# A Perceiver block on one core: the context's product for batches 2 to 14 by Strassen's scheme, with work moved between the vector engines

## The chip, the cores and the metric

The kernel runs on one core of a Trainium2 chip. The core has a matrix engine (TensorE, PE in the profile; its weight loads are PEld), three engines for element-wise work (VectorE or DVE, ScalarE or ACT, GpSimd or POOL), and SyncE (SP), which here only issues transfers. Each engine runs its own instructions in order; they wait for one another through semaphores. Matrix products read SBUF and write to PSUM, which has eight banks of 128 partitions x 512 float32 values. The metric is the time of one execution on the device in microseconds.

## The reference

Sixteen batches of 128 tokens with 512 features pass three stages; each adds to x what it makes of the normalised x. All is float32.

```python
# 1: cross-attention on the batch's own context, 2048 rows x 512
h      = layernorm(x)
probs  = softmax(h @ ctx.T)              # (128, 2048)
x      = x + probs @ ctx                 # "the context's product"
# 2: causal self-attention, 16 heads of 32; down- and up-projections, rotary half
x      = x + attention(layernorm(x), Wq, Wk, Wv) @ Wc
# 3: two of eight experts of rank 64, chosen by the first token
h      = layernorm(x)
x      = x + h + gates-weighted (h @ A.T) @ B.T
```

## The kernel before

**Tiling.** A batch is one tile of 128 tokens. The context of a batch is cut in four pieces v of 512 rows, and each piece in four chunks j of 128 rows. Both the context (`ctx`, rows on partitions) and its transpose (`ctxT`, features on partitions) are loaded for each piece, 1 MB each, by `load_ctx` and `load_turned`. The scores are made turned: `score` (L247) multiplies chunks of `ctxT` with the turned norm rows `hT` into a PSUM bank `psc`, so that context rows are on partitions and tokens along the bank. `keep_score` (L258) copies the bank to `sc` on ScalarE and keeps the running maximum `mx` on VectorE. `turn_max`, `most` and `spread` (L274 to 287) make from it the maximum of each token and spread it over the partitions with TensorE; `less` (L289) adds its negative on VectorE and `power` (L295) takes the exponential on ScalarE. `sums` (L298) adds the powers of each token, `whole` and `portion` finish the denominator. `attend` (L308) is the context's product: for each v, four matmuls with `sc` of a chunk (128 x 128) as weights and the chunk of `ctx` (128 x 512) as moving operand, all sixteen accumulated in one bank `av`. `x1_of` (L326) divides and adds x.

**Norms.** `Norm.moments` takes mean and variance on VectorE (`bn_stats`, `bn_aggr`) and the reciprocal root on POOL; `rows` applies them on VectorE; `turned` transposes 32x32 blocks on VectorE and sends the tile through DRAM and back (`d`, `hT`, on SP), which finishes the transposition.

**Self-attention.** `project` makes q and k, `rotate` and `rotated` apply the rotary part (VectorE and POOL), `project_v` makes v from the tokens in another order (`order_tokens`, POOL), `compare` makes the scores of all heads in four banks `pss` with row groups of 32, `powers` masks them, takes the maximum (VectorE) and the exponential with its sum (ScalarE, one instruction a head), `divided` divides on POOL, `turn_probs` transposes in 32x32 pieces on VectorE into `pT`, `heads` multiplies with v (`y`, four column groups of 32) and `join` with Wc (`o`). **Experts.** `shares`, `logit` and `choose` pick two experts, `fetch` gathers their weights by indirect transfers issued on POOL, `middle` (`mid`, weights of 64 columns for the two experts in turn) and `widen` (`ffn`) multiply, `end` adds and writes out.

**Order.** Every instruction is kept in program order (the class `InOrder`, L95), so each engine's queue is what the loop of L694 writes down. One pass of it handles three batches at once: self-attention of batch b, cross-attention's second half (less to x1) of a = b + 1, scores of s = b + 2, and the experts of l = b - 1. The order on TensorE in one pass is: q, spread, q, k, v, av (v = 0), pss, av, lg, av, den, av, psc, mid, psc, psc, ffn, y, psc, o. The last two batches are written out behind the loop.

**PSUM.** The eight banks are split in pools: `ps_sc` two, `ps_av` one, `ps_acc` five, each used in turn. All operations that go through `InOrder` carry line 101 in the profile, so they are told apart by the names of their tiles.

Of the kernel before, what the change touches and what calls it, by code (L numbers as in the profile page):

```python
# [66 lines left out]
def perceiver_block(ctx: ExitStack, tc: tile.TileContext, io: dict, out: bass.AP):  # L67
# [8 lines left out]
    ps_av = ctx.enter_context(tc.tile_pool(name="ps_av", bufs=1, space=PSUM))  # L76
    ps_acc = ctx.enter_context(tc.tile_pool(name="ps_acc", bufs=5, space=PSUM))
# [43 lines left out]
    class Norm:  # L121
        def __init__(self, src, name, n=P, tag="h", mixed=False, hT=None):
            self.src, self.name, self.n, self.tag, self.mixed, self.hT = src, name, n, tag, mixed, hT

        def moments(self):
            n = self.n
            stats = p2.tile([P, 6], F32, tag="stats", name=f"st_{self.name}")[:n]
            dve.bn_stats(stats, self.src)
            self.mv = p2.tile([P, 2], F32, tag="mv", name=f"mv_{self.name}")[:n]
            dve.bn_aggr(self.mv, stats)  # L130
            self.rstd = p2.tile([P, 1], F32, tag="rstd", name=f"rs_{self.name}")[:n]
            pool.tensor_scalar_add(self.rstd, self.mv[:, 1:2], EPS)
            pool.tensor_tensor(self.rstd, self.rstd, mhalf[:n], ALU.pow)
            return self

        def rows(self):
            of = p2 if self.tag == "h" else p1
            self.h = of.tile([P, D], F32, tag=self.tag, name=f"{self.tag}_{self.name}")[: self.n]
            to, of = self.h, self.src
            if self.mixed:  # L140
                to = to.rearrange("p (c a j) -> p c a j", c=KC, j=Q)
                of = of.rearrange("p (c j a) -> p c a j", c=KC, j=Q)
            dve.tensor_scalar(to, of, self.mv[:, 0:1], self.rstd, ALU.subtract, ALU.mult)
            return self
# [89 lines left out]
    norms, hTs = {}, {}  # L234
    scs, mxs, psc, parts, dens, rdens, avs, spreads, trs = ({} for _ in range(9))
# [3 lines left out]
    def norm1(b):  # L239
        norms[1, b] = Norm(xs[b], f"1_{b}", mixed=early(b), hT=(p2, "hT1")).moments()  # L240
# [6 lines left out]
    def score(b, v):  # L247
        ct, hT = turned_cts.pop((b, v)), hTs[1, b]
        ps = bank(ps_sc, "sc", f"psc_{b}_{v}").rearrange("p (j t) -> p j t", j=4)
        for j in range(4):  # L250
            for c in range(KC):
                matmul(
                    ps[:, j, :], ct[:, c, j * P : (j + 1) * P], hT[:, :, c, :],
                    start=(c == 0), stop=(c == KC - 1),
                )
        psc[b, v] = ps

    def keep_score(b, v):  # L258
        if v == 0:
            scs[b] = p2.tile([P, VC, 4, S], F32, tag="sc", name=f"sc_{b}")  # L260
            mxs[b] = p1.tile([P, 4, S], F32, tag="mx", name=f"mx_{b}")
        sc, mx, ps = scs[b], mxs[b], psc.pop((b, v))
        act.copy(sc[:, v], ps)
        if v:
            dve.tensor_tensor(mx, ps, mx if v > 1 else sc[:, 0], ALU.max)
        if v == VC - 1:
            dve.tensor_tensor(mx[:, :2], mx[:, :2], mx[:, 2:], ALU.max)
            dve.tensor_tensor(mx[:, 0], mx[:, 0], mx[:, 1], ALU.max)
# [5 lines left out]
    def turn_max(b):  # L274
        trs[b] = bank(ps_acc, "acc", f"tr_m_{b}")
        transpose(trs[b][:, :S], mxs.pop(b)[:, 0], ident)

    def most(b):
        nm = p2.tile([P, 1], F32, tag="nm", name=f"nm_{b}")
        dve.tensor_reduce(nm, trs.pop(b)[:, :S], AX.X, ALU.max, negate=True)  # L280
        diag = p1.tile([P, S], F32, tag="diag", name=f"diag_{b}")
        dve.tensor_scalar(diag, ident, nm, None, ALU.mult)
        trs[b] = diag
# [14 lines left out]
    def sums(b, by=dve):  # L298
        sc = scs[b]
        t = p1.tile([P, 4, S], F32, tag="sums", name=f"sums_{b}")  # L300
        for v in range(1, VC):
            by.tensor_tensor(t, sc[:, v], t if v > 1 else sc[:, 0], ALU.add)
        part = p2.tile([P, S], F32, tag="part", name=f"part_{b}")
        by.tensor_tensor(t[:, :2], t[:, :2], t[:, 2:], ALU.add)
        by.tensor_tensor(part, t[:, 0], t[:, 1], ALU.add)
        parts[b] = part

    def attend(b, v):  # L308
        sc, ct = scs[b], cts.pop((b, v))
        if v == 0:  # L310
            avs[b] = bank(ps_av, "av", f"av_{b}")
        for j in range(4):
            matmul(
                avs[b], sc[:, v, j, :], ct[:, j, :],
                start=(v == 0 and j == 0), stop=(v == VC - 1 and j == 3),
            )
# [9 lines left out]
    def x1_of(b):  # L326
        x1s[b] = p2.tile([P, D], F32, tag="x1", name=f"x1_{b}")
        dve.scalar_tensor_tensor(x1s[b], avs.pop(b), rdens.pop(b), xs.pop(b), ALU.mult, ALU.add)
        norms[2, b] = Norm(x1s[b], f"2_{b}", mixed=b in (0, B - 1), hT=(p1, "hT2")).moments()
# [33 lines left out]
    def order_tokens(b):  # L363
        hTvs[b] = p1.tile([P, KC, S], F32, tag="hTv", name=f"hTv_{b}")
        pool.tensor_copy(
            hTvs[b].rearrange("p c (i b) -> p c i b", i=Q),
            hTs[2, b].rearrange("p i c b -> p c i b"),
        )
# [8 lines left out]
    def keep_v(b):  # L377
        values[b] = p2.tile([P, D], F32, tag="vv", name=f"vv_{b}")
        act.copy(values[b], projected.pop(("v", b)))

    def compare(b):
        qT, kT = turned_qk.pop(("q", b)), turned_qk.pop(("k", b))
        pss = [bank(ps_acc, "acc", f"pss_{b}_{j}") for j in range(4)]
# [14 lines left out]
    def powers(b, g):  # L398
        att, nmx, sm, rsm, pss = atts[b]
        hs = slice(4 * g, 4 * g + 4)  # L400
        dve.tensor_tensor(
            att[:, hs, :],
            pss[g].rearrange("p (h t) -> p h t", h=4),
            cst[:, None, C_MASK : C_MASK + S].to_broadcast([P, 4, S]),
            ALU.add,
        )
        dve.tensor_reduce(nmx[:, hs], att[:, hs, :], AX.X, ALU.max)
        dve.tensor_scalar_mul(nmx[:, hs], nmx[:, hs], -SCALE)
        for i in range(hs.start, hs.stop):
            act.activation(  # L410
                att[:, i, :], att[:, i, :], AF.Exp,
                bias=nmx[:, i : i + 1], scale=SCALE, accum_out=sm[:, i : i + 1],
# [49 lines left out]
    def x2_of(b):  # L462
        x2s[b] = p2.tile([P, D], F32, tag="x2", name=f"x2_{b}")
        dve.tensor_tensor(x2s[b], os_.pop(b), x1s[b], ALU.add)
        norms[3, b] = Norm(x2s[b], f"3_{b}", mixed=late(b), hT=(p2, "hT3")).moments()
# [50 lines left out]
    def fetch(b):  # L516
        blocks, picked, ex = chosen[b]
        spare = b == B - 1
        each = (p2 if spare else p1).tile(
            [P, TOP, KC * R], F32, tag="sc" if spare else "each", name=f"each_{b}"  # L520
# [6 lines left out]
        wb = p2.tile([P, D], F32, tag="wb", name=f"wb_{b}")  # L527
# [15 lines left out]

    state = {}
# [13 lines left out]
    def first_joined(b):  # L558
# [3 lines left out]
        row = p1.tile([1, D], F32, tag="sums", name=f"row_{b}")  # L562
# [131 lines left out]
    for b in range(B - 2):  # L694
        l, a, s = b - 1, b + 1, b + 2
        if b:
            turn_max(a)
            project(b, "q", [0])
            most(a)
            x2_of(l)  # L700
            spread(a)
            project(b, "q", [1, 2, 3])
            order_tokens(b)
            less(a, 0)
            power(a, 0)
            rows(3, l)
            turn(3, l)
            less(a, 1)
            power(a, 1)
            residual(l)  # L710
            load_x(s + 1)
            load_turned(s, 2)
            less(a, 2)
            power(a, 2)
        else:
            project(b, "q")
        rotate(b, "q")
        project(b, "k")
        if b:
            less(a, 3)  # L720
            power(a, 3)
            load_turned(s, 3)
        rotated(b, "q")
        rotate(b, "k")
        project_v(b)
        keep_v(b)
        rotated(b, "k")
        attend(a, 0)
        load_ctx(a + 1, 0)
        compare(b)  # L730
        if b:
            sums(a)
            shares(l)
        powers(b, 0)
        attend(a, 1)
        load_ctx(a + 1, 1)
        powers(b, 1)
        if b:
            logit(l)
            choose(l)  # L740
        divided(b, 0)
        if b:
            fetch(l)
        attend(a, 2)
        powers(b, 2)
        divided(b, 1)
        whole(a)
        portion(a)
        powers(b, 3)
        divided(b, 2)  # L750
        if b:
            gate(l)
        load_ctx(a + 1, 2)
        attend(a, 3)
        divided(b, 3)
        x1_of(a)
        score(s, 0)
        turn_probs(b, 0)
        rows(2, a)
        turn(2, a)  # L760
        keep_score(s, 0)
        if b:
            middle(l)
        for i in (1, 2):
            turn_probs(b, i)
        score(s, 1)
        turn_probs(b, 3)
        keep_score(s, 1)
        load_ctx(a + 1, 3)
        score(s, 2)  # L770
# [3 lines left out]
        load_turned(s + 1, 0)  # L774
        heads(b)
        keep_heads(b)
        keep_score(s, 2)
        score(s, 3)
        if s + 1 < B:
            norm1(s + 1)  # L780
        load_turned(s + 1, 1)
        if s + 1 < B:
            rows(1, s + 1)
            turn(1, s + 1)
# [6 lines left out]
    project(y, "q", [0])  # L791
    most(z)
    x2_of(l)
    spread(z)
    project(y, "q", [1, 2, 3])
    order_tokens(y)
    less(z, 0)
    power(z, 0)
    rows(3, l)
    turn(3, l)  # L800
    for v in (1, 2, 3):
        less(z, v)
        power(z, v)
# [140 lines left out]
```

## Time and profile before

| | |
|---|---|
| median of three runs | 811.38 us (811.08 to 811.56) |
| profiled execution | 812.89 us |
| its span, first to last instruction | 811.1 us |
| granted TensorE clock over the span | 0.995 |
| PE, DVE, ACT, POOL busy in one batch of the loop (a window of 48 us) | 48.0, 37.0, 13.2, 14.5 us |
| HBM read and written | 165.5 and 15.2 MB |

Busy time is the time in which an engine executes something. A float32 matmul appears as two rows[...], so counts of PE are twice those of the source. A group's line gives the operation, what it writes and reads, its shape and count, then the busy time and the mean of one in ns, then the idle time of the engine just before it. In the chain of work that ended last, each piece has its start, its length, and how many rows it has.

### The profile page before, as it was taken

To read this page: it belongs to the slowest core of one execution; us is meant where nothing else is said; L and a number is where in the kernel's file an instruction comes from. 1 tells how busy PE (TensorE), PEld (TensorE's weight loads), DVE (VectorE), ACT (ScalarE), POOL (GpSimd) and SP (SyncE) were. 2 spreads that over 40 slices of the span, in tenths; PEclk is the share of its full clock that TensorE was granted. 3 is DMA by queue.
4 is the path that set the end of the run, shared out by engine and by line. 5 is a ranking of instruction groups with operands and counts; after the bars stand their busy time and mean duration, and the time that the engine had idled before them with its cause. 6 is when DMAs were issued, how large, how long until landed. Compare 5 with 4: busy or idle time off the path is not lost.

```text
span 811.1 us, 14245 instructions
## 1 busy us (share of the span) xinstructions
PE 793.7 (98%) x5506; PEld 570.6 (70%) x5506; DVE 581.7 (72%) x1289; ACT 223.6 (28%) x731; POOL 233.6 (29%) x295
## 2 busy tenths in 40 slices
PE   8999999999999999999999999999999999999985
PEld 8946785858677586867858686785868768586743
DVE  1446777787887778778777877877787777767673
ACT  1222323132142313214231321423132141313341
POOL 2001224133232403323240332324123232305333
PEclk9999999999999999999999999999999999999998
DMA  9989557567565856646585674658566565720001
GB/s 353 389 314 407 223 202 295 221 246 271 179 228 203 288 221 241 269 179 218 211 298 220 227 277 166 230 210 306 216 224 265 197 213 212 296 93 27 27 27 65
DMA packets 57971, 181.61 MB, mean 224 GB/s; under 512 B 5504, under 2 KB 27392, under 8 KB 41520
## 3 DMA queue, kind: packets, MB, share of 16 engines
q1 hardware_dynamic: 53760, 168.38, 55.9%
q0 software_dynamic: 4000, 12.26, 4.0%
q8 instruction: 43, 0.70, 0.3%
q14 instruction: 24, 0.20, 0.1%
q10 hardware_dynamic: 144, 0.07, 0.0%
HBM read 165.48 MB, written 15.20 MB: 223 GB/s over the span
## 4 chain that ended last, share of the span: by engine, by line
PE 96%; DVE 2%; DMA 1%; issue 0%; ACT 0%; POOL 0%; DVEq 0%; ACTq 0%
PE psc L101 29%; PE av L101 28%; PE q L101 7%; PE k L101 7%; PE o L101 7%; PE v L101 6%; PE pss L101 2%; PE mid L101 2%; PE ffn L101 2%; PE y L101 2%; PE spread L101 1%; PE tr L101 0%; PE tr_p L101 0%; DVE h L101 0%; DMA each<-in_A_dram,g_blocks 0%
## 5 line engine op out<-in xcount | busy, mean ns | idle before, releaser
L101 PEld LDWEIGHTS psc<-hT,ctxT 128*128 128x128 f32 x2048 | 234.7, 193 | 12.8 <-issue 9.1
L101 PE MATMUL psc<-hT,ctxT 128*128 128x128 f32 x2048 | 240.2, 277 | 0.7 <-ACT hT L101 0.7
L101 PE MATMUL av<-ctx,sc 128*128 128x512 f32 x512 | 232.9, 600 | 0.0
L101 PEld LDWEIGHTS av<-ctx,sc 128*128 128x128 f32 x512 | 93.6, 190 | 102.1 <-issue 100.3
L101 ACT ACTIVATE att<-att,nmx 128x128 f32<-128x128 f32 x256 | 99.2, 389 | 116.9 <-DVE nmx L101 114.6
L101 POOL TENSOR_TENSOR att<-att,rsm 128x512 f32<-128x512 f32 x60 | 61.2, 1041 | 166.3 <-DVE rsm L101 166.0
L101 DVE STREAM_TRANSPOSE pT<-att 32x512 f32<-32x512 f32 x140 | 98.3, 702 | 12.2 <-POOL att L101 10.3
L101 ACT COPY sc<-psc 128x512 f32<-128x512 f32 x64 | 37.6, 587 | 159.0 <-PE psc L101 159.0
L101 ACT ACTIVATE sc<-sc 128x512 f32<-128x512 f32 x64 | 39.7, 631 | 134.9 <-DVE sc L101 134.9
L101 POOL TENSOR_SCALAR rs<-mv 128x1 f32<-128x1 f32 x48 | 10.8, 226 | 185.4 <-DVE mv L101 183.6
L101 PEld LDWEIGHTS q<-hT,w_q 128*128 128x128 f32 x512 | 59.6, 192 | 4.1 <-issue 4.0
L101 PE MATMUL q<-hT,w_q 128*128 128x128 f32 x512 | 62.2, 275 | 0.0
L101 PE MATMUL k<-hT,w_k 128*128 128x128 f32 x512 | 59.8, 275 | 0.0
L101 PEld LDWEIGHTS k<-hT,w_k 128*128 128x128 f32 x512 | 58.5, 192 | 0.0
L101 PE MATMUL o<-w_c,yT 128*128 128x512 f32 x128 | 57.9, 594 | 0.0
L101 PE MATMUL v<-w_v,hTv 128*128 128x512 f32 x128 | 57.7, 593 | 0.0
L101 DVE TENSOR_TENSOR att<-pss,cst 128x512 f32<-128x512 f32 x64 | 43.3, 677 | 18.1 <-PE pss L101 18.1
L101 DVE TENSOR_SCALAR h<-x,mv,rs 128x512 f32<-128x512 f32 x48 | 33.0, 688 | 27.1 <-POOL rs L101 27.1
L101 POOL DMA_DIRECT2D out_dram<-x x14 | 9.2, 659 | 136.7 <-DVE x L101 136.7
L101 ACT ACTIVATION_READ_ACCUMULATOR att<-att,nmx 128x1 f32 x256 | 47.8, 187 | 0.0
L101 DVE TENSOR_REDUCE nmx<-att 128x4 f32<-128x512 f32 x64 | 43.9, 686 | 2.2
L101 DVE TENSOR_TENSOR mx<-psc,mx 128x512 f32<-128x512 f32 x32 | 21.6, 675 | 30.7 <-ACT sc L101 30.7
(132 smaller groups left out, 830.8 us busy)
## 6 DMA issues: line engine op xcount, KB each, us to landing
ctxT<-in_ctxT_dram SPq DMA_DIRECT2D x64, 1024.0 KB
ctx<-in_ctx_dram SPq DMA_DIRECT2D x64, 1024.0 KB
d<-turn SPq DMA_DIRECT2D x42, 256.0 KB
hT<-d SPq DMA_DIRECT2D x42, 256.0 KB
x<-in_x_dram SPq DMA_DIRECT2D x16, 256.0 KB
out_dram<-x POOLq DMA_DIRECT2D x14, 256.0 KB, 5.4
down_q<-in_Wq_downT_dram SPq DMA_DIRECT2D x2, 1024.0 KB
down_k<-in_Wk_downT_dram SPq DMA_DIRECT2D x2, 1024.0 KB
```

The costliest lines, as they stand in the source:

```text
L101: return lambda *args, **kwargs: tc.keep_in_program_order(issue(*args, **kwargs))
```

## The change

The product of batches 2 to 14 (`by_halves`) is computed by a Strassen-like scheme with seven products in place of eight. The tokens are cut in halves of 64, each v's rows in halves of 256 (two chunks each), the features in halves of 256. `context_halves` makes, on POOL, four differences of 128x512 for each v: one in place in `ctx`, three in a new tile `more`. `token_halves` makes four combinations of `sc` in a tile `blocks`, three on VectorE and one on POOL, for all four v at once. `attend_halves` issues fourteen matmuls for a v with 64 columns of weights and 256 moving columns, alternating between PSUM partitions 0 to 63 and 64 to 127 of two banks; part 0 needs no `blocks`, part 1 does. `attended` and `joined` put the parts together: three copies of half the partitions on ScalarE and five additions on VectorE. Batches 0, 1 and 15 keep the old product.

Beside it: norm rows of most batches are applied on ScalarE (`by_act`, with a shift made on POOL), the diagonal of `most` and the copy of `order_tokens` go to ScalarE, the folds of `mx` and the sums of the powers are one `tensor_reduce` each, the scaling of the maxima in `powers` goes into `scalar_tensor_tensor` and `negate`. PSUM is split anew (`ps_av` two, `ps_acc` four; two of the `pss` banks come from `ps_sc`), `sc`, `vv`, `part` and `wb` have one buffer in place of two, and the order of a pass is written anew: v is followed at once by pss; all of av comes behind it, in the pieces seen below; shares, fetch, residual and the turn of norm 3 come later in the pass.

```diff
     def keep_score(b, v):
         if v == VC - 1:
-            dve.tensor_tensor(mx[:, :2], mx[:, :2], mx[:, 2:], ALU.max)
-            dve.tensor_tensor(mx[:, 0], mx[:, 0], mx[:, 1], ALU.max)
+            most = p1.tile([P, S], F32, tag="most", name=f"most_{b}")
+            dve.tensor_reduce(most, mx.rearrange("p j t -> p t j"), AX.X, ALU.max)
     def rows(self):
+            if self.by_act:
+                act.activation(to, of, AF.Identity, bias=self.shift, scale=self.rstd)
+                return self
     def sums(b, by=dve):
+        if by is dve:
+            dve.tensor_reduce(part, sc.rearrange("p v j t -> p t (v j)"), AX.X, ALU.add)
+            return
+    HT, HD = S // 2, D // 2
+    def by_halves(b):
+        return 1 < b < B - 1
+    def context_halves(b, v, by=pool):
+        b11, b12, b21, b22 = (ct[:, 2 * k : 2 * k + 2, n * HD : (n + 1) * HD] for k in (0, 1) for n in (0, 1))
+        more = p4.tile([P, 3, 2, HD], F32, tag="more", name=f"more_{b}_{v}")
+        by.tensor_tensor(more[:, 1], b22, b12, ALU.subtract)
+        by.tensor_tensor(b12, b12, b11, ALU.subtract)
+        by.tensor_tensor(more[:, 0], b22, b12, ALU.subtract)
+        by.tensor_tensor(more[:, 2], b21, more[:, 0], ALU.subtract)
+    def token_halves(b):
+        t = p1.tile([P, 4, VC, 2, HT], F32, tag="blocks", name=f"blocks_{b}")
+        dve.tensor_tensor(t[:, 0], a21, a22, ALU.add)
+        dve.tensor_tensor(t[:, 2], a11, a21, ALU.subtract)
+        dve.tensor_tensor(t[:, 1], t[:, 0], a11, ALU.subtract)
+        pool.tensor_tensor(t[:, 3], a12, t[:, 1], ALU.subtract)
+    def attend_halves(b, v, parts=(0, 1)):
+        if 0 in parts:
+            of_k = [(
+                (low, left, one, sc[:, v, k, low], ct[:, k, left]),
+                (high, left, two, sc[:, v, 2 + k, high], more[:, 2, k]),
+            ) for k in range(2)]
+        if 1 in parts:
+            of_k += [(
+                (low, left, two, sc[:, v, 2 + k, low], ct[:, 2 + k, left]),
+                (high, left, one, t[:, 1, v, k], more[:, 0, k]),
+                (low, right, two, t[:, 3, v, k], ct[:, 2 + k, right]),
+                (high, right, two, t[:, 0, v, k], ct[:, k, right]),
+            ) for k in range(2)]
...
+    def joined(b):
+        dve.tensor_tensor(e[HT:, 0], one[HT:, :HD], moved[HT:, 0], ALU.add)
+        dve.tensor_tensor(moved[HT:, 1], one[HT:, HD:], moved[HT:, 1], ALU.add)
+        dve.tensor_tensor(e[HT:, 1], two[HT:, HD:], e[HT:, 0], ALU.add)
+        act.copy(first[:HT, 1], e[HT:, 1])
+        dve.tensor_tensor(
+            first[HT:], e[HT:, :1].to_broadcast([HT, 2, HD]),
+            moved[HT:, 1:].to_broadcast([HT, 2, HD]), ALU.add,
+        )
+        dve.tensor_tensor(e, two.rearrange("p (n d) -> p n d", n=2), first, ALU.add)
     def powers(b, g):
-        dve.tensor_tensor(
+        dve.scalar_tensor_tensor(
...
-        dve.tensor_reduce(nmx[:, hs], att[:, hs, :], AX.X, ALU.max)
-        dve.tensor_scalar_mul(nmx[:, hs], nmx[:, hs], -SCALE)
+        dve.tensor_reduce(nmx[:, hs], att[:, hs, :], AX.X, ALU.max, negate=True)
```

The order of a pass after the change, cut to what the steps below speak of:

```python
project(b, "k"); rotate(b, "k"); turn(3, l); project_v(b); rotated(b, "q"); rotated(b, "k")
compare(b)
attend(a, 0, (0,)); attend(a, 1, (0,)); token_halves(a); context_halves(a, 3)
powers(b, 0); attend(a, 0, (1,)); powers(b, 1); divided(b, 0); powers(b, 2); shares(l); divided(b, 1)
attend(a, 1, (1,)); logit(l); powers(b, 3); load_ctx(a + 1, 0); load_ctx(a + 1, 1)
choose(l); divided(b, 2); sums(a); attend(a, 2); load_ctx(a + 1, 2); divided(b, 3)
fetch(l); residual(l); gate(l); attend(a, 3); load_ctx(a + 1, 3); whole(a); attended(a)
turn_probs(b, 0); turn_probs(b, 1); joined(a); portion(a); x1_of(a); norm1(s + 1); score(s, 0)
turn_probs(b, 2); rows(2, a); turn(2, a); score(s, 1); turn_probs(b, 3); rows(1, s + 1); turn(1, s + 1)
context_halves(a + 1, 0); context_halves(a + 1, 1); score(s, 2); middle(l); score(s, 3, [0, 1])
heads(b); widen(l); end(l); keep_heads(b); context_halves(a + 1, 2); score(s, 3, [2, 3]); join(b)
```

## The prediction

> **What bounds the kernel now.** First the head of the page and its chain of work that ended last.
>
> ```profile
> PE 793.7 (98%) x5506; PEld 570.6 (70%) x5506; DVE 581.7 (72%) x1289; ACT 223.6 (28%) x731; POOL 233.6 (29%) x295
> PE 96%; DVE 2%; DMA 1%; issue 0%; ACT 0%; POOL 0%; DVEq 0%; ACTq 0%
> PE psc L101 29%; PE av L101 28%; PE q L101 7%; PE k L101 7%; PE o L101 7%; PE v L101 6%; PE pss L101 2%; PE mid L101 2%; PE ffn L101 2%; PE y L101 2%; PE spread L101 1%; PE tr L101 0%; PE tr_p L101 0%; DVE h L101 0%; DMA each<-in_A_dram,g_blocks 0%
> ```
>
> TensorE is the chain for 96% of the span, and the context's product, av, is 28% of it. So what av takes less is gained, if nobody else becomes late. Second, the same chain in order of time for one batch of the loop, and the line of the windows for it (PE, PEld, DVE, ACT, POOL busy us; clock):
>
> ```profile
> 427.50 7.34 PE psc L101 x64
> 435.71 1.01 PE y L101 x32
> 447.90 3.57 PE k L101 x32
> 451.48 3.44 PE v L101 x8
> 454.91 3.43 PE av L101 x8
> 458.35 1.10 PE pss L101 x32
> 459.45 3.63 PE av L101 x8
> 463.20 3.54 PE av L101 x8
> 466.85 3.54 PE av L101 x8
> 470.39 3.57 PE psc L101 x32
> 473.96 1.02 PE mid L101 x16
> 474.99 1.09 PE psc L101 x8
> 427.00:475.00 48.00, 48.00 (x340) 34.65 (x336) 37.03 (x82) 13.15 (x45) 14.47 (x18) 1.00 0.63 231
> ```
>
> A batch takes 474.99 - 427.50 = 47.49 us, without a gap on PE, at full clock. One float32 matmul is two rows here: 32 rows of k in 3.57 us is 0.1116 us for a row of 128 columns, 8 rows of v in 3.44 is 0.430 for 512; on the line between them a row of 256 takes 0.2177.
>
> **The change on TensorE.** Before, one v of av is 8 rows of 128x512: 8 x 0.430 = 3.44. After, it is 14 matmuls with 64 columns of weights and 256 moving ones, 28 rows. Alone, 28 x 0.2177 = 6.10. But they alternate between the lower and the upper 64 PSUM partitions, and mid, which does the same (64-column weights, alternating i), shows what that gives: 16 rows in 1.02 us, where 16 x 0.1116 one after another would be 1.79, and two at a time 0.89. y, with four groups of 32 columns and a different moving operand in each, does 32 rows in 1.01 (0.89 four at a time). So two streams with different moving operands do run together: 14 x 0.2177 = 3.05 for a v. Saved: 4 x (3.44 - 3.05) = 1.56 us a batch.
>
> Against it stands a rule of the Trainium skill, "TensorEngine Tiling (Array Packing)", Key Properties: changing the tiling mode drains TensorE. The row: mid's 1.02 less 0.89 is 0.13 for one excursion in and out. The new order has two more (halves of v 0 and 1, then lg in full width, then v 2 and 3, then den): +0.26. By a full drain with the next weights loaded bare it could be twice that, 0.52 (one more 0.13 each); I take the row. PE alone: 47.49 - 1.56 + 0.26 = 46.19 a batch.
>
> **The change on the other engines, per batch.** DVE, from the rows:
>
> ```profile
> L101 DVE TENSOR_REDUCE nmx<-att 128x4 f32<-128x512 f32 x64 | 43.9, 686 | 2.2
> L101 DVE TENSOR_SCALAR h<-x,mv,rs 128x512 f32<-128x512 f32 x48 | 33.0, 688 | 27.1 <-POOL rs L101 27.1
> L101 DVE TENSOR_TENSOR sums<-sc,sums 128x512 f32<-128x512 f32 x30 | 20.8, 692 | 3.0
> L101 DVE TENSOR_TENSOR mx<-mx 128x256 f32<-128x256 f32 x16 | 6.8, 425 | 0.6
> L101 POOL TENSOR_TENSOR qP<-qP,cst 128x512 f32<-128x512 f32 x15 | 19.1, 1272 | 21.0 <-DVE qP L101 21.0
> L101 POOL TENSOR_TENSOR sums<-sc,sums 128x512 f32<-128x512 f32 x2 | 2.9, 1432 | 0.2
> ```
>
> Away: three norm rows 2.07, diag 0.29, the folds of mx 0.42 + 0.29, of sums 0.68 + 2 x 0.69 + 0.42 + 0.29, four scalings of nmx 4 x 0.17: 6.5. Added: token_halves 3 x 0.69, joined 3 x 0.42 (64x256, by the 256-element row) + 2 x 0.69, the reduce of mx 0.69, the reduce of sums over 2048 elements, and 4 x 0.07 for scalar_tensor_tensor (750 ns beside tensor_tensor's 677). A reduce of 2048 has no row: 686 ns is some 0.15 fixed and 0.53 for 512, so 2.3; strided reading has none either, and twice, 4.5, is my upper end; 2.3 is taken, since the transposes of the 32-wide pieces of att (702 ns) cost no more than of whole rows (711). Added: 7.9. DVE 36.6 -> 38.0 of 46.2. ACT gains three norm rows (0.63 each), diag 0.37, hTv 0.59 and three half copies (0.58 + 2 x 0.40): 13.2 -> 17.4, off the chain. POOL loses hTv (0.60) and gains 16 subtractions of 512 elements and one more in token_halves at 1.27, and three shifts at 0.24: 14.5 -> 36.2. DMA moves the same bytes. Costed at nothing, with their cover: the ctx loads of the next batch follow on SP when a v has been multiplied, 11 to 17 us after the end of k, and POOL reads the first at 26; turn(3) moves behind k, so that its write and read (2.1 us between their issues, before too) have some 8 us until shares; fetch moves behind sums, and its gathers (4.8 us to landing by the page) are issued from 17 to 21, for mid at 28; the banks of ps_acc, four now, are each read out over 2 us before their next turn. Should one of these be late, the next to wait is the PE group named, for the same time.
>
> **Does PE wait?** No engine is full, so it is the order that decides. Count from the end of k. PE until y: v 3.44, pss 1.10, av 4 x 3.05 + 0.26, lg and den 0.24 + 0.2 of changes, three psc 10.81, mid 1.02, half a psc 1.89: 31.2 us. In that stretch DVE has (next starts 0.62 after the one before where nothing depends, about 0.72 where it does): signal and kP, kT, turn, qT, kT to 3.4 (pss, at 3.5, waits for this); blocks 2.1 (5.5); two powers 2.7 (8.2); the first reciprocal when four exponentials of 0.385 are done (8.6); powers, shares, powers 3.3 (11.9; lg needs shares at 10.4 and comes at about 10.7); choose 1.55, reduce 2.3, the last reciprocal (15.9); the last divided on POOL (17.0); three transposes of 0.714 (19.2); joined 2.75 (21.9); x1 and two sets of moments (24.6); three transposes, turn, mx, four transposes 6.35: 30.95. So y, pss and lg are each met with 0.1 to 0.3 us to spare. These are races that I can't call to 0.3 us; as the mean wait I take 0.15 a batch.
>
> POOL: its third input of the second halves, 1.27 after DVE's blocks at 5.5, is ready at 6.8; PE asks for it 0.43 into that part, at 4.74 + 1.74 + 0.43 = 6.9. Then the subtractions of v 3 (5.1) to 11.9 are ahead of divided, whose last reciprocal comes at 15.9: four times 1.04 ends at 17.0 as above. Then three fetches (1.25 each by their starts in the trace), residual 1.3; two roots and shifts behind DVE's moments to 26.0; v 0 and 1 of the next batch (10.3), the output's issue 0.7, v 2 (5.1), root 1.2: 43.3; qP to 44.8; kP is needed to start at 46.2 + 1.5. Spare: 2.9 us over 12 subtractions.
>
> Here the second rule bears, "SBUF — State Buffer", Who interferes with whom: a VectorE instruction with two SBUF inputs locks GpSimd's reads out for its whole length. In the changed order the long runs of subtractions lie beside transposes, mx (one PSUM input), less, x, reduces; none has two SBUF inputs but shares (0.2 us). By the row (1.27, taken beside such work before) and by the rule the sum is the same; were every subtraction to wait for one VectorE operation of 0.7, it would be 1.97.
>
> **The sum.** 46.19 + 0.15 = 46.34, 1.15 less a batch. The halves run for batches 2 to 14, that is 13 passes (b = 1 to 13): 15.0 us. Start, pass 0 and the last two batches keep their products; reordering there I put at 0, within 1 us either way. On the profiled execution, span 811.1 in 812.9 us, that gives a span of 796.1; the median of the runs, 811.38, lies 1.5 below that execution's time, and 811.4 - 15.0 = 796.4: **796.5 us**. With no wait and no switch price it is 811.4 - 13 x 1.56 = 791; with 0.52 for switches and 0.5 of waits, 13 x 0.54 = 7 off, 804.
>
> **Rivals.** *VectorE's stretch becomes the bound* (chance 0.15). It has 0.2 us to spare against 31.2. For: three points met so closely. If it is 0.7 to 1.2 us longer than summed (each hand-over 0.1 more), PE waits 0.5 to 1.0 and 4 to 10 us remain: 801 to 808, say 804. Against: I counted DVE's rows at their means.
> *POOL is locked out* (0.12, the slower side). Place: the 12 subtractions between the roots and kP. At 1.97 each they take 8.4 us more, of which 2.9 is hidden; PE waits 5.5 at pss; 5.5 - 1.15 = 4.35 a batch, 868. It decides from (2.9 + 1.15) / 12 = 0.34 more, 1.61 us each. For: POOL goes from 30% to 78% busy and its slowest row is 1.43. Against: 1.43 is still hidden (12 x 0.16 = 1.9), and the two-SBUF operations stand elsewhere.
> *The halves don't run together* (0.02): 6.10 a v, +2.66, 52 of them: 950. mid and y speak against it.
> *PE's gain is just eaten* (0.03), 810 to 813: waits of about 1.3 a batch.
>
> **How the numbers follow.** The likeliest, PE-bound with small waits, has 0.68 and its own range 790 to 804. With the first rival it gives faster 0.83. Same 0.03, within 0.2% (1.6 us, about what a measurement of this kernel can tell). Slower 0.14. The range runs from 790 to 809; that leaves the two slower cases, the even one and little else outside.
>
> **What would show it.** av rows of 64-column weights whose starts lie near 0.11 us apart, 0.22 for a pair; a batch of 46.2 to 46.5 between equal psc pieces; PE 97% busy or more; POOL subtractions at 1.27; the reduce of sums at 2.3; no waits above 0.5 at pss, lg, y. Wrong: subtractions above 1.6 with kT waiting for POOL's kP; a reduce of 4.5 (then y is 2.0 late, and the change loses); av starts at 0.22 apart.

## The result: 841.7 us, 3.7% slower

The changed kernel takes 841.71 us (840.19 to 843.17), the kernel before 811.47 on the same chip; the ratio is 1.037 (95% interval 1.0345 to 1.0392). The forecast was 796.5, with 790 to 809 as its range.

The head of the page of the changed kernel and its chain of work that ended last:

```profile
PE 779.7 (93%) x6546; PEld 595.2 (71%) x6546; DVE 652.7 (78%) x1196; ACT 282.0 (34%) x841; POOL 516.5 (62%) x544
PE 40%; DVE 40%; issue 11%; POOL 4%; ACT 3%; DMA 1%; DVEq 0%; POOLq 0%; ACTq 0%
```

PE has 14 us less to do, but it makes up only 40% of the chain in place of 96%; another 40% runs over VectorE. VectorE's busy time is 652.7 us of 838.4, so it is not full either. What sets the pass is an order in which two engines wait for each other in turn. One pass as a window (PE, PEld, DVE, ACT, POOL busy; clock; DMA):

```profile
414.10:463.60 49.50, 46.38 (x412) 36.23 (x411) 41.99 (x77) 17.34 (x53) 36.17 (x38) 1.00 0.63 221
```

A pass takes 49.50 us in place of 47.49: 13 x 2.0 = 26 of the 27.3 us by which the spans differ. ACT (17.3) and POOL (36.2) have what was summed; VectorE has 42.0 where the sum said 38.0. The first two lines here are from the kernel before, the others from the changed one:

```profile
L101 DVE TENSOR_TENSOR g_share<-w_r,hT 128x32 f32<-128x32 f32 x15 | 3.1, 205 | 1.4 <-ACT hT L101 1.4
L101 DVE TENSOR_SCALAR g_blocks<-g_at,cst 128x2 int32<-128x2 f32 x16 | 3.7, 228 | 0.6
L101 DVE TENSOR_REDUCE part<-sc 128x128 f32<-128x2048 f32 x15 | 55.4, 3693 | 0.7 <-ACT sc L101 0.7
L101 DVE TENSOR_TENSOR first<-x,moved 64x512 f32<-64x512 f32 x13 | 31.3, 2405 | 0.0
L101 DVE TENSOR_REDUCE most<-mx 128x128 f32<-128x512 f32 x16 | 16.8, 1047 | 0.5
L101 DVE TENSOR_TENSOR g_share<-w_r,hT 128x32 f32<-128x32 f32 x15 | 13.9, 928 | 1.8 <-ACT hT L101 1.8
L101 DVE TENSOR_SCALAR g_blocks<-g_at,cst 128x2 int32<-128x2 f32 x16 | 12.5, 780 | 0.6
L101 POOL TENSOR_TENSOR more<-ctx 128x512 f32<-128x512 f32 x104 | 132.6, 1275 | 4.4
```

Five rows are longer than counted: the reduce of the sums (3.69 us, counted 2.3), `first` (2.40, counted 0.69), the reduce of mx (`most`, 1.05, counted 0.69), `g_share` (0.93 in the mean, 0.21 before), `g_blocks` (0.78, 0.23 before). `most` lies between the last scores and `tr_m`, where PE does not wait in the passes. The subtractions on POOL take the 1.27 that was counted. Where PE waits, from the list of waits (total us, times, longest):

```profile
PE psc L101 <- DVE mx L101: 17.5, 13, 1.5
PE y L101 <- DVE pT L101: 10.9, 13, 0.8
PE den L101 <- DVE g_dn L101: 9.3, 13, 0.7
PE lg L101 <- DVE rsm L101: 3.0, 14, 0.6
```

All are waits for VectorE, once in each of the 13 passes, together 3.1 us a pass. The largest is at psc: the scores of v = 3 need one of the two banks of `ps_sc` again, and VectorE's mx has to read it first. For den and lg the profile names a small operation near in time; by the program the first needs `part`, the second `g_part`, which end just ahead of those.

### The profile page after: what moved, and what is told of

The parts are those of the page before. It is cut to its first block, busy times and chain, and to the rows that moved or that the text cites. A ratio compares the mean times of both kernels' runs of the same rounds, so it can differ in the third digit from the quotient of the medians.

```text
span 838.4 us, 16727 instructions
## 1 busy us (share of the span) xinstructions
PE 779.7 (93%) x6546; PEld 595.2 (71%) x6546; DVE 652.7 (78%) x1196; ACT 282.0 (34%) x841; POOL 516.5 (62%) x544
## 4 chain that ended last, share of the span: by engine, by line
PE 40%; DVE 40%; issue 11%; POOL 4%; ACT 3%; DMA 1%; DVEq 0%; POOLq 0%; ACTq 0%
DVE pT L101 9%; PE psc L101 8%; PE o L101 7%; PE k L101 6%; PE q L101 6%; PE av L101 5%; DVE x L101 4%; DVE first L101 4%; DVE nmx L101 3%; POOL att L101 3%; DVE att L101 3%; DVE blocks L101 3%; ACT att L101 3%; DVE st L101 2%; DVE kT L101 2%
## 5 line engine op out<-in xcount | busy, mean ns | idle before, releaser
L101 PE MATMUL av<-ctx,sc 128*64 128x256 f32 (+1 forms) x512 | 150.6, 422 | 0.0
L101 POOL TENSOR_TENSOR more<-ctx 128x512 f32<-128x512 f32 x104 | 132.6, 1275 | 4.4
L101 PEld LDWEIGHTS av<-ctx,sc 128*64 128x64 f32 (+1 forms) x512 | 72.6, 147 | 48.2 <-issue 19.9
L101 PE MATMUL av<-more,blocks 128*64 128x256 f32 x416 | 91.1, 379 | 0.0
L101 POOL TENSOR_TENSOR more<-ctx,more 128x512 f32<-128x512 f32 x52 | 66.3, 1275 | 4.1
L101 POOL TENSOR_TENSOR ctx<-ctx 128x512 f32<-128x512 f32 x52 | 66.2, 1273 | 4.1
L101 PE MATMUL av<-ctx,blocks 128*64 128x256 f32 x416 | 62.6, 379 | 0.0
L101 ACT ACTIVATE h<-x,sh,rs 128x512 f32<-128x512 f32 x41 | 33.4, 814 | 75.0 <-POOL sh L101 74.4
L101 DVE TENSOR_REDUCE part<-sc 128x128 f32<-128x2048 f32 x15 | 55.4, 3693 | 0.7 <-ACT sc L101 0.7
```

The source lines that it names most:

```text
L101: return lambda *args, **kwargs: tc.keep_in_program_order(issue(*args, **kwargs))
```

## Experiments

The theory: the stretch of VectorE from the end of k to the last piece of pT, which PE's y needs, is longer than PE's own way there. It is too long because the reduce reads with a stride, and because operations with two SBUF inputs are held up while POOL reads SBUF. The rivals: `first` and the reduce are simply slow in any case; POOL is late, not its port; PE's halves cost more than counted; one of the other edits is at fault. Each kernel is compared with runs of the kernel before on its own chip (medians of 812.95 and 813.09 us there).

### residual moved behind the turns

```diff
             fetch(l)
-            residual(l)
             gate(l)
...
             turn(1, s + 1)
+        if b:
+            residual(l)
         context_halves(a + 1, 0)
```

> The changed kernel with residual (POOL, two SBUF inputs, 1.28 us) behind the roots and turns in place of behind fetch, so that it no longer starts while VectorE's addition `first` waits. Port theory: first falls from 2.40 us to 0.7, at most 1.3 if the gathers' issue holds it too; x1 and all behind it on VectorE come 1.1 to 1.7 us earlier, and 13 passes give 14 to 22 us: 820 to 828. Rival, that an addition of 64 partitions with two repeated operands simply takes 2.4: first stays 2.4 and the time 840 to 843.

Measured: 820.0 us (819.8 to 822.4), and a pass of 47.88. `first`, and the POOL instruction that ran across it:

```profile
L101 DVE TENSOR_TENSOR first<-x,moved 64x512 f32<-64x512 f32 x13 | 9.0, 691 | 0.0
431.61 0.95 POOL L101 DMA_INDIRECT wb<-in_BT_dram,g_rows  x1 [0.30 <-issue]
432.01 0.69 DVE L101 TENSOR_TENSOR first<-x,moved 64x512 f32<-64x512 f32 x1
```

`first` takes 0.69 us, with a gather being issued on POOL across it. So it was residual, with its two inputs in SBUF, that held it up. In the changed kernel's timeline both engines show it:

```profile
438.24 2.40 DVE L101 TENSOR_TENSOR first<-x,moved 64x512 f32<-64x512 f32 x1
437.83 0.95 POOL L101 DMA_INDIRECT wb<-in_BT_dram,g_rows  x1 [0.30 <-issue]
438.81 1.28 POOL L101 TENSOR_TENSOR x<-x,h 128x512 f32<-128x512 f32 x1
```

residual ends at 440.09, `first` 0.55 later at 440.64: a wait and then its own work. Moving one instruction gave some 21 us, 1.6 a pass, and PE's wait at psc is gone with it.

### The sums read in the order of memory

```diff
-            dve.tensor_reduce(part, sc.rearrange("p v j t -> p t (v j)"), AX.X, ALU.add)
+            dve.tensor_reduce(part, sc.rearrange("p v j t -> p (v j t)").rearrange("p (t n) -> p t n", t=S), AX.X, ALU.add)
```

> The changed kernel with the reduce of the powers reading 16 neighbouring elements for each of its 128 sums in place of 16 elements 512 bytes apart; it adds other elements, so the denominators are other ones. Stride theory: 2048 elements take 2.2 to 2.4 us in place of 3.69, VectorE's stretch shortens by 1.4, and the time is 841.7 - 13 x 1.4 = 823 to 826. Rival, that 2048 elements into 128 sums take 3.7 in any order: 841 to 843.

Measured: 821.9 us (821.2 to 823.4), a pass of 48.08.

```profile
L101 DVE TENSOR_REDUCE part<-sc 128x128 f32<-128x2048 f32 x15 | 33.9, 2259 | 0.7 <-ACT sc L101 0.7
L101 DVE TENSOR_TENSOR first<-x,moved 64x512 f32<-64x512 f32 x13 | 31.3, 2404 | 0.0
```

The same count of elements and sums takes 2.26 us, what the forecast had counted; the other 1.43 are the stride of 512 bytes. They come back one for one in the pass (49.50 to 48.08), and `first` is as long as it was.

### The last reciprocal ahead of the sums

```diff
-        if b:
-            sums(a)
         attend(a, 2)
         load_ctx(a + 1, 2)
         divided(b, 3)
+        if b:
+            sums(a)
```

> The changed kernel with the last reciprocal of divided issued on VectorE before the reduce of the powers, not behind it. If VectorE's stretch from k to y sets the pass, the wait of POOL's last division behind the reduce (2.6 us) goes, and of it what is not used up by the reduce itself: the reduce then runs while POOL divides, so that the transposes start 1.0 to 1.1 us earlier; 13 passes: 826 to 829. If TensorE or POOL set it, no change: 841 to 843.

Measured: 812.2 us (810.4 to 815.7), ratio 0.9988 (0.9971 to 1.0005), a pass of 47.21. That is 2.3 us a pass, twice what was expected. The timeline tells why:

```profile
463.93 3.69 DVE L101 TENSOR_REDUCE part<-sc 128x128 f32<-128x2048 f32 x1
464.03 2.04 POOL L101 TENSOR_TENSOR att<-att,rsm 128x512 f32<-128x512 f32 x2 [0.68 <-DVE rsm L101]
469.83 1.29 POOL L101 TENSOR_TENSOR x<-x,h 128x512 f32<-128x512 f32 x1
471.39 0.69 DVE L101 TENSOR_TENSOR first<-x,moved 64x512 f32<-64x512 f32 x1
467.77 0.35 PE L101 MATMUL den<-ones,part 128*128 128x1 f32 x2 [0.78 <-DVE g_dn L101]
```

POOL divides while VectorE reduces, as expected. With that POOL is through with residual at 471.12, just before `first` begins, so that wait goes too: two causes with one edit. What is left is PE's 0.78 at den, for the sums.

### No reading in context_halves

```diff
-        by.tensor_tensor(more[:, 1], b22, b12, ALU.subtract)
-        by.tensor_tensor(b12, b12, b11, ALU.subtract)
-        by.tensor_tensor(more[:, 0], b22, b12, ALU.subtract)
-        by.tensor_tensor(more[:, 2], b21, more[:, 0], ALU.subtract)
+        by.memset(more, 0.0)
+        by.memset(more, 1.0)
+        by.memset(more, 0.0)
```

> The changed kernel with context_halves writing constants: three memsets of 1536 elements on POOL in place of four subtractions; the differences of the context are left out, so the product is another. POOL writes as long (about 1.4 us each) but reads no SBUF there. Port theory: g_share falls from 0.93 to 0.2, g_blocks[...] may stay near 0.8 or fall to 0.23, first stays 2.4 (its wait is for residual and the gathers); VectorE's stretch shortens by 0.7 to 1.4: 823 to 833. Rival, that POOL's lateness and not its port sets the pass: POOL has 1 us less to do in each v, with the same effect on kP; g_share stays 0.9.

Measured: 831.5 us (830.3 to 833.1), a pass of 48.70.

```profile
418.10 4.25 POOL L101 MEMSET more<- 128x1536 f32 x3
421.14 0.20 DVE L101 TENSOR_TENSOR g_share<-w_r,hT 128x32 f32<-128x32 f32 x1
424.41 0.23 DVE L101 TENSOR_SCALAR g_blocks<-g_at,cst 128x2 int32<-128x2 f32 x1
L101 DVE CAST g_at<-g_best 128x2 f32<-128x2 uint32 x16 | 11.4, 712 | 0.6
```

The same operation in the changed kernel, beside a subtraction:

```profile
425.32 1.04 DVE L101 TENSOR_TENSOR g_share<-w_r,hT 128x32 f32<-128x32 f32 x1
425.01 1.28 POOL L101 TENSOR_TENSOR more<-ctx 128x512 f32<-128x512 f32 x1
```

`g_share` runs in 0.20 us in the middle of POOL's writing; beside the subtraction it takes 1.04 and ends at 426.36, just behind the subtraction (426.29). So an operation with two SBUF inputs is held up by a POOL instruction that reads SBUF, and not merely because POOL is busy. `g_blocks` is at 0.23 too, but it met POOL idle here (its divisions ended at 424.35). The wait has moved one operation ahead: `g_at`, a cast of two elements that takes 0.17 us in the changed kernel, now takes 0.71 in the mean, since it is the one that lies beside a division (in this pass from 423.54 to 424.38). The 0.8 us a pass are therefore those of `g_share`.

### The old product with all other edits

```diff
     def by_halves(b):
-        return 1 < b < B - 1
+        return False
```

> The changed kernel with by_halves false for every batch: the old product of sixteen matmuls, all other edits kept (no differences, no blocks, no joined). TensorE needs 47.4 us a pass, VectorE has 2.0 (blocks) and 4.9 (joined with its wait) less in its stretch, which is 34.8 long in the changed kernel; so TensorE sets the pass except for the wait for the sums before den. If the stretch is the cause: 811 to 822. If one of the other edits costs the time by itself: over 830.

Measured: 815.2 us (814.4 to 816.8), ratio 1.0025 (1.0014 to 1.0035), a pass of 47.40. So the other edits together neither win nor lose in the pass. With no subtractions POOL is busy for 29% of the span; `g_share` and `g_blocks` are back at 0.20 and 0.23, while the reduce is still 3.66, hidden there. What this kernel takes more lies outside the passes: in the two profiled executions (816.8 and 812.9 us) the way to the first pass's k is 1.6 us longer than before, the 13 passes are 0.8 shorter, and what follows is 3.1 longer.

### Choosing the experts without a port in common

```diff
-        dve.tensor_scalar(blocks, at, float(P), column(C_P), ALU.mult, ALU.add)
+        for i in range(TOP):
+            dve.tensor_scalar(blocks[:, i : i + 1], at[:, i : i + 1], float(P), column(C_P), ALU.mult, ALU.add)
...
-    def context_halves(b, v, by=pool):
+    def context_halves(b, v, by=pool, between=None):
...
         by.tensor_tensor(b12, b12, b11, ALU.subtract)
+        if between:
+            between()
         by.tensor_tensor(more[:, 0], b22, b12, ALU.subtract)
...
-        context_halves(a, 3)
+        context_halves(a, 3, between=(lambda: share_of(l, by=pool)) if b else None)
```

`share_of` is the product of `shares`; the reduce of `shares` stays on VectorE. The last reciprocal stays ahead of the sums here and in the next two kernels.

> sum_behind_reciprocal, and the product g_share on POOL (between the second and third difference of v = 3) in place of VectorE, and g_blocks as two operations of one element. Port theory: 0.83 us at g_share and some 0.4 at g_blocks leave VectorE's stretch to the sums, which is 0.8 us late before den; so den comes 0.8 us earlier, lg and pss stay: 47.2 - 0.8 to 1.0 a pass, 13 passes 10 to 13 us below sum_behind_reciprocal, 799 to 802. If the waits were only shown there and came from elsewhere: 811.

Measured: 797.5 us (796.8 to 798.1), ratio 0.980 (0.9778 to 0.9825). Two passes of its chain and the group:

```profile
392.78 3.57 PE k L101 x32
439.01 3.57 PE k L101 x32
L101 DVE TENSOR_SCALAR g_blocks<-g_at,cst 128x1 int32<-128x1 f32 x32 | 5.4, 210 | 0.6
```

A pass takes 46.23 us, 1.0 less than with the reciprocal alone, and PE's wait at den is gone. `g_blocks` takes 0.21 for each of two single elements, though POOL divides beside both (they run from 408.38 to 408.72, the divisions from 408.28 to 412.32). The two edits were not run apart, so how they share the gain is not shown. Between the profiled executions the gain is 12.9 us, as expected; the medians, taken on two chips, lie 14.7 apart.

### The sums in two steps

```diff
+    def fold(b):
+        t = p1.tile([P, 2, 4, S], F32, tag="first2", name=f"fold_{b}")
+        dve.tensor_tensor(t, scs[b][:, :2], scs[b][:, 2:], ALU.add)
+        folds[b] = t
...
+            dve.tensor_reduce(part, t.rearrange("p v j t -> p t (v j)"), AX.X, ALU.add)
...
         rotate(b, "q")
+        if b:
+            fold(a)
         project(b, "k")
```

`first` and `moved` share the tile of `fold`, which is free by then.

> sum_behind_reciprocal, and the sums in two steps: one addition of 2 x 1024 elements on VectorE while it waits for k (1.22 us in a gap of 1.65), and the reduce over 1024. Stride theory: the reduce falls from 3.69 to 1.9, den waits no longer, 0.8 us a pass and 10 us in all: 801 to 803; if the addition delays qP on POOL (both read two SBUF inputs) by 1.2, kP and pss come up to 0.2 later: 804. No stride effect: the same as sum_behind_reciprocal, 811.

Measured: 805.3 us (804.3 to 806.5), a pass of 46.83.

```profile
L101 DVE TENSOR_REDUCE part<-fold 128x128 f32<-128x1024 f32 x13 | 25.2, 1941 | 0.0
L101 DVE TENSOR_TENSOR first<-x,first 64x512 f32<-64x512 f32 x13 | 26.7, 2050 | 0.0
PE y L101 <- DVE pT L101: 4.5, 12, 0.4
```

The reduce falls to 1.94 as expected and PE no longer waits at den. But VectorE is now early enough to meet residual again: `first` is back at 2.05, and y waits 0.4. So half of the 0.8 us a pass is lost again, and the time lies above the expected 801 to 804. The other risk, qP held up by the addition, does occur (up to 2.25 us), but PE waits at pss no more than in the changed kernel (1.4 us, once).

### Both

> Both edits over sum_behind_reciprocal. VectorE's stretch is then 3 us shorter than where it met TensorE 0.8 us late, TensorE sets the pass at 46.2 to 46.4: 811.5 - 13 x 1.2 = 796, 794 to 799. If TensorE's own halves cost more than counted, it stays near 800 to 803 with PE's waits gone.

Measured: 799.6 us (797.3 to 801.3), ratio 0.984 (0.9817 to 0.986). The chain of one pass, in order of time:

```profile
396.41 3.44 PE v L101 x8
399.85 1.10 PE pss L101 x32
400.95 6.19 PE av L101 x56
407.14 0.32 PE lg L101 x2
407.46 6.19 PE av L101 x56
413.66 0.31 PE den L101 x2
413.97 10.83 PE psc L101 x96
424.80 1.02 PE mid L101 x16
425.82 1.98 PE psc L101 x16
427.81 1.08 PE y L101 x32
```

PE has no gap; a pass takes 46.23 us, as in swap_choose, and the runs of the two overlap. The median lies a little above the expected 794 to 799; the profiled execution (797.3) and the pass do not. `first` takes 2.28 here and costs nothing, since PE does not get to y before pT is done. swap_choose is the smaller edit and the best version found: 797.5 us, 2.0% below the kernel before and 5% below the changed one.

## Why the prediction was wrong, by its own steps

**TensorE's part was right.** All_three shows it alone: the product takes 2 x 6.19 = 12.38 us (forecast 4 x 3.05 + 0.26 = 12.46), from the end of k to y PE needs 427.81 - 396.41 = 31.4 (31.2), and a pass 46.23 (46.19 for PE alone). Pairs of rows start 0.22 us apart. The price of a change of tiling mode came out near the forecast. Before, lg and den stood in the chain with 0.12 us each:

```profile
463.08 0.12 PE lg L101 x2
466.74 0.12 PE den L101 x2
```

In all_three they take 0.32 and 0.31. Taken together, av, lg and den need 13.01 us in place of 14.38. The forecast's two sums differ here by 0.2: the one for the pass leaves 14.38 - 1.56 + 0.26 = 13.08, the one to y has 12.90, and the measured time lies between. A doubled drain did not appear.

**The step that failed is the sum of VectorE's stretch from k to y**, 30.95 us, on which "with 0.1 to 0.3 us to spare" and a mean wait of 0.15 rested. In the changed kernel (k ends at 415.83, y begins at 450.47) it was 34.6. From the end of k, in us:

| until | forecast | measured |
|---|---|---|
| the last powers | 11.9 | 12.1 |
| choose | 13.5 | 14.3 |
| the sums and the last reciprocal | 15.9 | 18.1 |
| three transposes | 19.2 | 21.4 |
| joined | 21.9 | 25.6 |
| the last transpose, y | 30.95 | 34.6 |

The difference of 3.7 stands in three places. *The reduce*: 3.69 for 2.3. The stride had been named as unknown, with 4.5 as the upper end, and settled by transposes of 32-wide pieces; that was the wrong row, since the reduce reads single elements 512 bytes apart. It is worth 1.4 a pass (sum_contiguous). *joined*: `first` 2.40 for 0.69, held by residual; 1.6 a pass (residual_late). *shares and choose*: 0.83 at `g_share` and some 0.7 at `g_blocks`; only 0.8 of this shows in the table, mainly since VectorE had run 0.3 to 0.5 us ahead of the forecast until then (blocks end 5.05 us after k, forecast 5.5). PE's way is 31.2 long, so it waits 34.6 - 31.2 = 3.4; 46.19 + 3.4 = 49.6, and the pass is 49.50. Two thirds of the wait on record fall at psc and den (1.35 and 0.72 of 3.1 us), two points that the forecast's list of close meetings (y, pss, lg) does not have.

**The rule of the Trainium skill, "SBUF — State Buffer", Who interferes with whom, held; its use did not.** It was looked up for the long runs of subtractions alone, and for POOL being delayed. There the sum was right: 1.275 us each, and kP never late. But in this trace VectorE waits too. The two-input operations of VectorE that lay beside the short POOL pieces were not listed: `first` beside residual, `g_share` beside a subtraction (named, and costed at 0.2, its own length, not at the length of what it waits for), `g_blocks` beside a division. For the last the page's other half would have told, that a `tensor_scalar` may take both ports when its operands allow it; the runs agree as far as they go, 0.78 us for two elements beside a division and 0.21 for one. That it is this form, no run shows.

**The rivals.** The first, VectorE's stretch as the bound, is what happened; its price was cut off at 1.2 us too long where 3.7 came. It should have been the rival on the slower side: it needs only 1.3 us more than PE's way to eat the gain. POOL locked out (868) did not happen: the subtractions keep their 1.27, and at kP, where this rival had POOL late, POOL waits for VectorE:

```profile
416.66 1.27 POOL L101 TENSOR_TENSOR kP<-kP,cst 128x512 f32<-128x512 f32 x1 [1.13 <-DVE kP L101]
```

That the halves don't run together did not happen.

**What would show it wrong** was named rightly in one case: a reduce of 4.5 would make y 2.0 late and lose the gain; 3.69 cost 1.4 a pass.

## What to carry to other kernels

When a change takes time from the engine that bounds, add up the longest chain of the next engine through the same stretch, and price each of its new rows by one that reads memory in the same pattern. An operation that another engine's reading can hold up cost, in these traces, its own length and the rest of what the other was doing: list, for each two-input operation, which reading instruction of the other engine can be under way. Where two such chains interlock, a swap of two instructions can be worth more than the arithmetic saved: here 2.3 us a pass against 1.3.

## What the runs showed of the hardware

- A reduce over elements 512 bytes apart costs (3.69 - 1.94) / 1024 = 1.7 ns an element, and `most` with its 512 elements fits: (1.94 - 1.05) / 512 = 1.7. Over neighbours it is (2.26 - 0.69) / 1536 = 1.0 ns, with the reduce to nmx (0.69 us for 512 elements) as the short one.
- `g_share`, an operation of 32 elements, took 1.04 us beside a POOL subtraction and 0.20 beside a POOL memset.
- `first` waited for residual although its shown start was 0.57 us ahead of residual's (438.24 and 438.81), with a gather's issue under way between; beside a gather's issue alone it did not wait. What decides the order in that moment, no run tells.
- The wait goes the other way as well. In 8 of the 13 passes of all_three POOL's qP starts 0.1 us behind VectorE's addition of 1024 elements and takes 2.24 us; in four it starts when the addition has ended and takes 1.27, as in the changed kernel. In the first pass qP was 0.4 us ahead, and the addition took 1.96 us in place of 1.2. One of the eight:

```profile
394.72 1.24 DVE L101 TENSOR_TENSOR fold<-sc 128x1024 f32<-128x1024 f32 x1
394.84 2.24 POOL L101 TENSOR_TENSOR qP<-qP,cst 128x512 f32<-128x512 f32 x1
```
